# Fold, first column and product u in another order within the slots of a selective scan

## The chip, the cores and the metric

The kernel runs on one core of a Trainium2 chip. The metric is the device time of one execution in microseconds (us); less is better. The engines are named as in the profile: PE is TensorE (PEld are its weight loads), DVE is VectorE, ACT is ScalarE, POOL is GpSimd, and SP is SyncE, which here issues nearly all DMAs. Each engine works through its own instructions in order, and waits for others by semaphores.

## The reference: what is computed

Layer 0 takes x (16 images, 96 channels, 64 x 64): a 1x1 convolution, then in every 8x8 window the 9 nearest neighbours of each pixel by cosine distance, an edge convolution with gelu, a maximum over the neighbours, another 1x1 convolution and a residual. Layer 1 runs two Mamba blocks over the 4096 pixels of each image as a sequence, and then a fusion convolution, a batch norm and a residual. The part that the change touches is the selective scan of a Mamba block:

```
delta = softplus(dt @ dt_w + dt_b)                 # 192 channels
dA  = exp(delta[..., None] * A)                    # 16 states for each channel
dBx = delta[..., None] * B[:, :, None, :] * xc[..., None]
h_t = dA_t * h_(t-1) + dBx_t                       # over the sequence
y   = sum over states of h * C, plus Dp * xc
```

## The kernel before

Each image is cut into 8 rows of 512 pixels. Layer 0 works on one row at a time; a Mamba block (layer i = 0 or 1 of image b, row k) on such a row is an **item** n. There are 256 items, and the two blocks alternate, block 1 four rows behind block 0.

An item has 8 **slots**, p = 0 to 7, one for each pair of states: 128 partitions hold 64 channels for each of two states, and the free dimension holds 3 groups of channels times 512 pixels. There are 2048 slots; m counts them. In slot m the following is written, in this order, and each engine sees its own part of it in this order:

- PE: the **broadcast** of B for slot m + 1 into the one PSUM tile bt (`bcast`, L792). It must wait until the product of slot m has read bt.
- DVE: the **scan** of slot m (L990) over da and db into a tile hb, of which there are 3.
- All engines: one step of each generator that is under way. These hold layer 0 (`nearest`, `edges`), the norm and the projections of the item after next (`norm`, `prelude`), the start values of the next item (`carry`) and the end of the last one (`tail`). ACT's exponentials da (L758) and the DMAs of C (ct, L751) are written two slots ahead (`chosen`). PE writes products into two PSUM buffers that ACT must empty.
- In slot 7 only, POOL: `restart(*after)`, the first column for slot 0 of the next item.
- DVE: the **product** db = u * bt for slot m + 1 (`times_b`, L798).
- PE: the **fold** of slot m - 1 (`folded`, L814 and L816): it adds hb, already multiplied by C, into the item's y in PSUM. In slot 1 a new y is begun (`skipped`), and the fold of slot 0 is put off until behind the broadcast of slot 2.
- POOL: a copy of the last column of hb as state (L1024), then **hb times ct**, the product with C (L1025).
- POOL: `restart`, the **first column** of u for slot m + 2 (L789), in all slots but 6. It overwrites a column of u that the product of slot m + 1 reads, and the product of slot m + 2 needs it.

In slot 4 of an item the prelude of the item after next begins; in slot 4 of the following one it writes ACT's softplus (L720, L721) with the eight DMAs of delta (`doubled`), then POOL's **product u**, up = sp * xc (L732), and in slot 5 the eight DMAs that spread up into u. `carry` reads u in slot 7.

Waiting lists (`between`, `later`, `late`, `closing`, `opening`) hold steps of layer 0 for a fitting place in a slot. Nothing plans at run time: the order of every engine's instructions is fixed by the order in which Python writes them.

Of the kernel before, what the change touches and what calls it, by code (L numbers as in the profile page):

```python
# [14 lines left out]
ALU = mybir.AluOpType  # L15
# [6 lines left out]
def tile_conv_knn_mamba(ctx: ExitStack, tc: tile.TileContext, w: dict, out: bass.AP):  # L22
# [8 lines left out]
    nc = tc.nc  # L31
# [22 lines left out]
    NPR = NS // 2  # L54
# [270 lines left out]
    later = [[], []]  # L325
    late = []
# [9 lines left out]
    def half(h):  # L336
        return slice(h * CB, (h + 1) * CB)
# [7 lines left out]
    def close_steps():  # L345
        while closing:
            products, use = closing.pop(0)
            uses.append(partial(use, products()))

    def open_steps():  # L350
        for several in (uses, opening):
            while several:
                several.pop(0)()
# [230 lines left out]
    def pooled(b):  # L584

        mean = pr.tile([C, 1], F32, tag="mean1", name=f"mean1_{b}")
        nc.vector.reduce_sum(mean, means.pop(b), AX.X)
        yield
        pg = pm.tile([C, 1], F32, tag="mm", name=f"pg_{b}")
        nc.tensor.matmul(pg, lhsT=gpT, rhs=mean, start=True, stop=True)  # L590
        yield
        gp = pr.tile([C, 1], F32, tag="gp", name=f"gp_{b}")
        nc.scalar.activation(gp, pg, AF.Relu, bias=gp_b[:, 0, :], scale=1.0 / L)
        yield
        def product():
            ps = pm.tile([C, 1], F32, tag="mm", name=f"pg2_{b}")
            nc.tensor.matmul(ps, lhsT=fusT[:, 1, :], rhs=gp, start=True, stop=True)
            return ps

        apart(product, lambda ps: nc.scalar.copy(gcol[:, b : b + 1], ps))  # L600
        yield


    PIECES = ((0, 2), (2, NB3))
    LAG = 4
    NR = NB * NQ
# [13 lines left out]
    def norm(n):  # L620

        b, i, k = items[n]
        nm = f"{b}_{i}_{k}"
        seq = seqs[b, k]
        assert (b, k) in done
        hn = hns[n % NHN]
        if k == 0:
            nc.gpsimd.memset(hn[:, :HALO], 0.0)
        else:
            nc.gpsimd.tensor_copy(hn[:, :HALO], hns[place[b, i, k - 1] % NHN][:, Q:])  # L630
        pc = pm.tile([C, Q], F32, tag="mm", name=f"pc_{nm}")
        nc.tensor.matmul(pc, lhsT=cmat, rhs=seq, start=True, stop=True)
        sq = pr.tile([C, Q], F32, tag="sq", name=f"sqv_{nm}")
        nc.scalar.activation(sq, pc, AF.Square)  # L634
        yield
        ps = pm.tile([C, Q], F32, tag="mm", name=f"pvar_{nm}")
        nc.tensor.matmul(ps, lhsT=ones_cc, rhs=sq, start=True, stop=True)
        rs = pr.tile([C, Q], F32, tag="rs", name=f"rs_{nm}")
        nc.scalar.activation(rs, ps, AF.Ln, bias=eps_t[:C], scale=1.0 / C)
        nc.scalar.activation(rs, rs, AF.Exp, scale=-0.5)  # L640
        yield
        nc.gpsimd.tensor_tensor(hn[:C, HALO:], seq, rs, ALU.mult)

    def prelude(n):
# [5 lines left out]
        xc = pr.tile([128, Q + QH], F32, tag="xc", name=f"xc_{nm}")  # L650
# [58 lines left out]
        sp = pr.tile([128, Q + QH], F32, tag="sp", name=f"sp_{nm}", bufs=1)  # L709
# [16 lines left out]
        up = pr.tile([128, Q + QH], F32, tag="up", name=f"up_{nm}", bufs=1)  # L726
# [2 lines left out]
            yield  # L729
        while pressed:  # L730
            pressed.pop(0)()
        nc.gpsimd.tensor_tensor(up, sp, xc, ALU.mult)  # L732
        yield
        doubled(u, up)

# [51 lines left out]
    def restart(n, p):  # L787

        nc.gpsimd.tensor_copy(made[n][5][:, :, 0], carried[n][:, :, p])  # L789

    def bcast(n, p):
        nc.tensor.matmul(bt[:, 1:], lhsT=bsel[:, p, :], rhs=made[n][2][:, 1:], start=True, stop=True)  # L792

    def times_b(n, p):
        parts = []
        for lo, hi in PIECES:
            db = pd.tile([128, hi - lo, Q], F32, tag=f"db{lo}", name=f"db{lo}_{n}_{p}")
# [13 lines left out]
    def folded(n, p, hb, y):  # L811

        for h in range(2):
            nc.tensor.matmul(y[half(h), 0], lhsT=fold, rhs=hb[:, h, :], start=False, stop=(p == NPR - 1))  # L814
        for h in range(2):
            nc.tensor.matmul(  # L816
                y[half(h), 1, :QH], lhsT=fold, rhs=hb[:, 2, bass.ts(h, QH)], start=False, stop=(p == NPR - 1)
            )
# [44 lines left out]
    def drain(*several):  # L863

        several = list(several)
        while several:
            next(loading, None)
            open_steps()
            several = [g for g in several if next(g, several) is not several]
            close_steps()  # L870
            for rest in (*later, late):
                while rest:
                    rest.pop(0)()
        open_steps()
# [10 lines left out]
    def several_at_once(g, pace):  # L885

        while True:
            made = 0
            while made < pace:
                step = next(g, g)  # L890
                if step is g:
                    return
                if step in (TABLE, SLOT):
                    break
                made += step is not SPARE
            yield step
# [14 lines left out]
    order = [(n, p) for n in range(NI) for p in range(NPR)]  # L911
# [3 lines left out]
    def ahead():  # L915
        if coming:
            t = coming.popleft()
            soon[t] = chosen(*t)
# [24 lines left out]
    y = behind = None  # L943
# [7 lines left out]
    for m, (n, p) in enumerate(order):  # L951
        b, i, k = items[n]
        nm = f"{b}_{i}_{k}"
        after = order[m + 1] if m + 1 < len(order) else None

        for layer0, r, pace in rows_at.pop(m, ()):
            steps = layer0(*divmod(r, NQ))
            going.append(several_at_once(steps, pace) if pace > 1 else steps)
        between.extend(later[0])
        later = [later[1], []]  # L960
        if p == 0 and k == 0:
            states[i] = pr.tile([128, NB3, NPR], F32, tag=f"state{i}", name=f"state_{nm}")
        if p == 0 and whole:
            going.append(pooled(whole.pop(0)))
        if p == 0 and n + 2 < NI:
            going.insert(0, norm(n + 2))
        if p == 4 and n + 2 < NI:
            preps.append(prelude(n + 2))
        if p == 6 and n + 1 < NI:
            going.append(carry(n + 1))  # L970
        ct, at = soon.pop((n, p))
        if after is not None:
            bcast(*after)
        if p == 2:
            folded(*put_off)


        while uses:
            uses.pop(0)()
        acts = list(opening)  # L980
        opening.clear()
        if not acts and between and p not in (0, 1):
            acts.append(between.popleft())
        if len(acts) > 1:
            acts.pop(0)()
        for act in acts:
            act()
        hb = pr.tile([128, NB3, Q], F32, tag="hb", name=f"hb_{nm}_{p}", bufs=3)
        for (lo, hi), part in zip(PIECES, db):
            nc.vector.tensor_tensor_scan(  # L990
                *(t.rearrange("p c q -> p (c q)") for t in (hb[:, lo:hi], das[at][:, lo:hi], part)), 0.0, ALU.mult, ALU.add
            )
        free.append(at)
        while late:
            if between:
                between.popleft()()
            else:
                late.pop(0)()
        if p == 1 and n:
            yc = emptied(n - 1, y)  # L1000
        if p == 7 and n:
            going.append(tail(n - 1))
        if p == 2:
            ahead()
        held = step_on(going)
        if p == 4:
            ahead()
        held |= step_on(preps)
        close_steps()
        if between and p in (4, 5):  # L1010
            between.popleft()()
        if after is not None:
            if p == NPR - 1:
                restart(*after)
            db = times_b(*after)
        if behind is not None:
            if p == 1:
                y = py.tile([128, 2, Q], F32, tag="y", name=f"y_{nm}")
                skipped(n, y)
                put_off = (*behind, y)  # L1020
            else:
                folded(*behind, y)
        if k + 1 < NQ:
            nc.gpsimd.tensor_copy(states[i][:, :, p : p + 1], hb[:, :, Q - 1 : Q])  # L1024
        nc.gpsimd.tensor_tensor(hb, hb, ct.unsqueeze(1).to_broadcast([128, NB3, Q]), ALU.mult)  # L1025
        if m + 2 < len(order) and p != NPR - 2:
            restart(*order[m + 2])
        if p == 1 and n:
            gate(n - 1, yc)
        behind = (n, p, hb)  # L1030
        while (not held or not soon) and len(soon) < AHEAD and coming:
            ahead()
# [68 lines left out]
```

## Time and profile before

| what | value |
|---|---|
| median of 3 runs | 12,521.8 us (12,520.07 to 12,522.95) |
| the profiled execution | 12,521.96 us |
| its span, first to last instruction | 12,520.2 us |
| granted TensorE clock, mean | 0.984 |
| busy: ACT, POOL | 82%, 80% |
| hb times ct (L1025) | 2048 times, 3454 ns each |
| product u (L732) | 256 times, 1813 ns each; POOL idle before it 443.1 us |
| first column (L789) | 2047 times, 212 ns each |
| scan (L990) | 2048 pairs, 6944.1 us in all |

The span covers everything but 1.8 us of the profiled execution, and that execution is within 0.2 us of the median. A group's line in the profile has the number of instructions, their busy time and mean duration, and the idle time of their engine just before them with what ended it. The end of a PE instruction is modelled, so starts are the safer numbers there.

### The profile page before, as it was taken

What the parts mean: (1) busy time and instruction counts of PE and PEld (TensorE: products, weight loads), DVE (VectorE), ACT (ScalarE), POOL (GpSimd) and SP (SyncE); (2) the same over time, 40 slices, a digit from 0 to 9 for tenths busy, and PEclk for the clock granted to TensorE, in tenths of its full rate; (3) what the DMA queues carried; (4) which work ended last, traced back from release to release, by engine and by line L of the source; (5) the groups of instructions that cost most, each with busy time, mean ns of one, the idle gap of its engine ahead of it and who ended that gap; (6) DMA issues with size and microseconds to landing.
All of it is one profiled execution on the core that took longest, in us unless ns stands there. A gap on an engine that the chain in (4) does not pass through costs nothing. (4 is left out here: it accounts for less than half of the span.)

```text
span 12520.2 us, 169034 instructions
## 1 busy us (share of the span) xinstructions
PE 11019.7 (88%) x50504; PEld 4348.2 (35%) x50504; DVE 11646.8 (93%) x10589; ACT 10249.1 (82%) x16756; POOL 10022.4 (80%) x10148
## 2 busy tenths in 40 slices
PE   7989899898999999899999989989999898998972
PEld 2333333333333333333333333333333333333320
DVE  3999999999999999999999999999999999999995
ACT  6888888888888888888888888888888888888863
POOL 2888888888888888888888888888888888888882
PEclk9999999999999999999999999999999999999996
DMA  1333333333333333333333333333333333333336
GB/s 38 90 86 94 88 90 93 85 92 90 89 92 88 92 91 88 92 91 87 93 89 89 93 86 93 91 89 92 87 93 91 86 93 88 90 93 86 93 92 270
DMA packets 1221003, 1169.01 MB, mean 93 GB/s; under 512 B 631456, under 2 KB 762926, under 8 KB 1213936
## 3 DMA queue, kind: packets, MB, share of 16 engines
q1 hardware_dynamic: 1212720, 1132.88, 33.8%
q10 hardware_dynamic: 7360, 25.32, 0.5%
q8 instruction: 397, 6.50, 0.2%
q14 instruction: 526, 4.31, 0.1%
HBM read 640.79 MB, written 93.09 MB: 59 GB/s over the span
## 5 line engine op out<-in xcount | busy, mean ns | idle before, releaser
L1025 POOL TENSOR_TENSOR hb<-hb,ct 128x1536 f32<-128x1536 f32 x2048 | 7074.4, 3454 | 692.0 <-DMA ct<-cd 448.0
L990 DVE TENSOR_TENSOR_SCAN hb<-da,db 128x1024 f32<-128x1024 f32 (+1 forms) x4096 | 6944.1, 1738 | 4.2 <-ACT da L758 4.2
L798 DVE TENSOR_TENSOR db<-u,bt 128x1024 f32<-128x1024 f32 (+1 forms) x4096 | 3711.4, 952 | 564.1 <-PE bt L792 201.0
L758 ACT ACTIVATE da<-delta,a 128x511 f32<-128x511 f32 x6144 | 3946.1, 710 | 15.9 <-DVE hb L990 8.2
L814 PE MATMUL y<-hb,fold 128*64 128x512 f32 x8192 | 2179.7, 610 | 41.2 <-POOL hb L1025 41.2
L516 ACT ACTIVATE da<-t,eb,es 128x512 f32<-128x512 f32 x1536 | 1168.3, 776 | 714.0 <-PE t L508 453.3
L816 PE MATMUL y<-hb,fold 128*64 128x256 f32 x8192 | 1244.0, 382 | 0.0
L508 PE MATMUL t<-oh,vu 128*128 128x512 f32 x2048 | 1006.4, 613 | 28.2 <-ACT da L516 26.6
L816 PEld LDWEIGHTS y<-hb,fold 128*64 128x64 f32 x8192 | 593.0, 138 | 1191.2 <-issue 1191.2
L1024 POOL COPY state<-hb 128x3 f32<-128x3 f32 x1792 | 374.6, 209 | 766.4 <-DVE hb L990 731.0
L447 DVE TENSOR_REDUCE hq<-da 128x192 f32<-128x1536 f32 x512 | 891.6, 1742 | 91.3 <-ACT da L516 91.3
L792 PE MATMUL bt<-bparts,bsel 128*128 128x511 bf16 x2048 | 796.0, 389 | 180.0 <-DVE db L798 176.6
L659 PE MATMUL pj<-hn,conv_in 128*128 128x512 f32 x2048 | 934.7, 599 | 18.4 <-ACT gcol L600 8.8
L814 PEld LDWEIGHTS y<-hb,fold 128*64 128x64 f32 x8192 | 507.9, 137 | 1078.1 <-issue 695.3
L511 PE MATMUL t<-oh,vu 128*64 128x512 f32 x2048 | 560.8, 626 | 311.6 <-ACT da L516 309.0
L732 POOL TENSOR_TENSOR up<-sp,xc 128x768 f32<-128x768 f32 x256 | 464.1, 1813 | 443.1 <-ACT sp L721 442.9
L664 PE MATMUL pj<-hn,conv_in 128*64 128x256 f32 x4096 | 498.9, 385 | 259.0 <-ACT xc L671 258.8
L671 ACT ACTIVATE xc<-pj,conv_b 128x512 f32<-128x512 f32 (+1 forms) x512 | 297.0, 580 | 425.3 <-PE pj L664 400.4
L477 ACT ACTIVATE oh<-off 64x512 f32<-64x512 bf16 x1024 | 638.2, 623 | 6.4
L492 PE MATMUL pv<-ewT,y 96*64 96x192 f32 x2048 | 447.0, 342 | 143.8 <-ACT sqv L634 83.2
L659 PEld LDWEIGHTS pj<-hn,conv_in 128*128 128x128 f32 x2048 | 378.6, 190 | 406.0 <-issue 368.7
L508 PEld LDWEIGHTS t<-oh,vu 128*128 128x128 f32 x2048 | 371.9, 193 | 394.9 <-issue 298.5
(188 smaller groups left out, 15801.1 us busy)
## 6 DMA issues: line engine op xcount, KB each, us to landing
ct<-cd SPq DMA_DIRECT2D x4096, 128.0 KB
delta<-sp SPq DMA_DIRECT2D x1024, 128.0 KB
u<-up SPq DMA_DIRECT2D x1024, 128.0 KB
delta<-sp SPq DMA_DIRECT2D x1024, 64.0 KB
u<-up SPq DMA_DIRECT2D x1024, 64.0 KB
x<-in_x SPq DMA_DIRECT2D x128, 192.0 KB
rn<-r4d SPq DMA_DIRECT2D x128, 192.0 KB
x_d<-x SPq DMA_DIRECT2D x128, 192.0 KB
```

Of the source, the lines that this page charges most:

```text
L447: nc.vector.tensor_reduce(out(), g.rearrange("p s (i k) -> p s i k", k=KO), AX.X, ALU.max)
L477: nc.scalar.activation(ohs[p][0:NN, h], off[half(h)], AF.Relu, bias=1.0, scale=-1.0)
L508: nc.tensor.matmul(t, lhsT=vus[p][:, part, :128], rhs=ohw[part], start=True, stop=True)
L516: nc.scalar.activation(g, t, AF.Gelu, bias=e_b[:, j : j + 1], scale=e_s[:, j : j + 1])
L659: nc.tensor.matmul(ps, lhsT=wt[:, t, :128], rhs=hn[:, off : off + Q], start=(t == 0), stop=(t == taps - 1))
L758: nc.scalar.activation(da[:, c, 1:Q], delta[:, c, 1:], AF.Exp, scale=a_neg[i][:, c, p : p + 1])
L792: nc.tensor.matmul(bt[:, 1:], lhsT=bsel[:, p, :], rhs=made[n][2][:, 1:], start=True, stop=True)
L798: nc.vector.tensor_tensor(db, made[n][5][:, lo:hi], bt.unsqueeze(1).to_broadcast([128, hi - lo, Q]), ALU.mult)
L814: nc.tensor.matmul(y[half(h), 0], lhsT=fold, rhs=hb[:, h, :], start=False, stop=(p == NPR - 1))
L816: nc.tensor.matmul(y[half(h), 1, :QH], lhsT=fold, rhs=hb[:, 2, bass.ts(h, QH)], start=False, stop=(p == NPR - 1))
L990: nc.vector.tensor_tensor_scan(*(t.rearrange("p c q -> p (c q)") for t in (hb[:, lo:hi], das[at][:, lo:hi], part)), 0.0, ALU.mult, ALU.add)
L1025: nc.gpsimd.tensor_tensor(hb, hb, ct.unsqueeze(1).to_broadcast([128, NB3, Q]), ALU.mult)
```

## The change

Three things move; no instruction is added or taken away.

1. The fold is always put off: a slot's fold is no longer written behind the next slot's product but at the start of the slot after, behind the broadcast. `HASTE` holds all 16 places, so the branch that folds at once is left only for the last slot of the program. Slots 2 and 10 of every 16 had this order already.
2. In slots 0 to 4 and 7 the first column for slot m + 2 is written ahead of the state copy and of hb times ct. In slot 5 it stays behind them; slot 6 has none. The column of slot 7 for the next item's slot 0 stays where it was.
3. The product up = sp * xc is put on a list (`behindhand`) and written behind hb times ct of the same slot, behind the first column too. The start of the program, which prepares the first items in `drain`, empties the list at the end of each round.

```diff
+    HASTE = {0,1,2,3,4,5,6,7,8,9,10,11,12,13,14,15,}
+    put_off = []
+    behindhand = []
...
-        nc.gpsimd.tensor_tensor(up, sp, xc, ALU.mult)
+        behindhand.append(lambda: nc.gpsimd.tensor_tensor(up, sp, xc, ALU.mult))
         yield
         doubled(u, up)
...
-            for rest in (*later, late):
+            for rest in (behindhand, *later, late):
...
         if after is not None:
             bcast(*after)
-        if p == 2:
-            folded(*put_off)
-
+        while put_off:
+            folded(*put_off.pop())
...
                 skipped(n, y)
-                put_off = (*behind, y)
-            else:
-                folded(*behind, y)
+            put_off.append((*behind, y))
+            if p != 1 and (m % 16 not in HASTE or after is None):
+                folded(*put_off.pop())
+        if m + 2 < len(order) and p < NPR - 3 or p == NPR - 1 and after is not None:
+            restart(*order[m + 2])
         if k + 1 < NQ:
             nc.gpsimd.tensor_copy(states[i][:, :, p : p + 1], hb[:, :, Q - 1 : Q])
         nc.gpsimd.tensor_tensor(hb, hb, ct.unsqueeze(1).to_broadcast([128, NB3, Q]), ALU.mult)
-        if m + 2 < len(order) and p != NPR - 2:
+        if p == NPR - 3:
             restart(*order[m + 2])
+        while behindhand:
+            behindhand.pop(0)()
```

## Prediction

> **What bounds the kernel now.** I read the page first, for the busy shares and the costliest groups. They point at the vector engine: it is busy 93%, and its product db = u times bt, which starts the work of every slot, has sat idle 564.1 us before it.
>
> ```profile
> PE 11019.7 (88%) x50504; PEld 4348.2 (35%) x50504; DVE 11646.8 (93%) x10589; ACT 10249.1 (82%) x16756; POOL 10022.4 (80%) x10148
> L798 DVE TENSOR_TENSOR db<-u,bt 128x1024 f32<-128x1024 f32 (+1 forms) x4096 | 3711.4, 952 | 564.1 <-PE bt L792 201.0
> ```
>
> Next I read the timeline of the vector engine. The loop repeats every 16 slots (two items and one row of layer 0). I number slots 0 to 15 within such a period, and db(8) is the product for slot 8. Here are db(1), db(8) and the next db(1) of two periods; the idle time stands in brackets.
>
> ```profile
> 4038.84 1.83 DVE L798 TENSOR_TENSOR db<-u,bt 128x1024 f32<-128x1024 f32 x2 [2.12 <-PE bt L792]
> ...
> 4078.57 1.83 DVE L798 TENSOR_TENSOR db<-u,bt 128x1024 f32<-128x1024 f32 x2 [0.17 <-POOL u L789]
> ...
> 4132.81 1.83 DVE L798 TENSOR_TENSOR db<-u,bt 128x1024 f32<-128x1024 f32 x2 [2.12 <-PE bt L792]
> ```
>
> ```profile
> 4513.36 1.83 DVE L798 TENSOR_TENSOR db<-u,bt 128x1024 f32<-128x1024 f32 x2 [2.07 <-PE bt L792]
> ...
> 4554.63 1.83 DVE L798 TENSOR_TENSOR db<-u,bt 128x1024 f32<-128x1024 f32 x2 [1.71 <-POOL u L789]
> ...
> 4607.32 1.83 DVE L798 TENSOR_TENSOR db<-u,bt 128x1024 f32<-128x1024 f32 x2 [1.38 <-POOL b L698]
> ```
>
> The period is 93.97 us in the one and 93.96 in the other, although POOL held the vector engine up by 0.17 us at db(8) in the first and by 1.71 in the second; what is lost at db(8) is missing from the next wait at db(1). The broadcast for slot 9 starts 44.43 us after that for slot 1 in both, and in 9 of 10 of the 121 full periods within 0.02 of that. So something that neither the vector engine nor POOL moves sets the period: TensorE and ScalarE, which wait for each other. The timelines of both in slots 2 and 3 show it.
>
> ```profile
> 6127.57 0.38 PE L792 MATMUL bt<-bparts,bsel 128*128 128x511 bf16 x1
> 6127.88 1.08 PE L814 MATMUL y<-hb,fold 128*64 128x512 f32 x4
> 6128.79 0.60 PE L816 MATMUL y<-hb,fold 128*64 128x256 f32 x4
> 6129.32 1.98 PE L508 MATMUL t<-oh,vu 128*128 128x512 f32 x4
> 6132.65 1.08 PE L511 MATMUL t<-oh,vu 128*64 128x512 f32 x4 [1.34 <-ACT da L516]
> 6133.56 1.03 PE L814 MATMUL y<-hb,fold 128*64 128x512 f32 x4
> 6134.42 0.60 PE L816 MATMUL y<-hb,fold 128*64 128x256 f32 x4
> 6134.95 0.39 PE L792 MATMUL bt<-bparts,bsel 128*128 128x511 bf16 x1
> 6135.18 1.88 PE L508 MATMUL t<-oh,vu 128*128 128x512 f32 x4
> ```
>
> ```profile
> 6133.78 0.78 ACT L516 ACTIVATE da<-t,eb,es 128x512 f32<-128x512 f32 x1 [0.51 <-PE t L511]
> 6136.24 0.78 ACT L516 ACTIVATE da<-t,eb,es 128x512 f32<-128x512 f32 x1 [1.68 <-PE t L508]
> ```
>
> ScalarE idles 1.68 us because TensorE, between two products of layer 0, does a fold (L814, L816) and a broadcast (L792). The same 1.68 stands in slot 11. I followed the rest of that period (6,119 to 6,213 us) back from one broadcast to the next: each step is TensorE waiting for ScalarE, ScalarE waiting for TensorE, or either busy; no step waits for DVE or POOL. TensorE does wait 176.6 us in all for db (mostly in slots 10 and 15), but ScalarE is later still there.
>
> **Fold behind broadcast.** In slots 2 and 10 the kernel already has this order; 14 of 16 slots change. The work between two products of layer 0 is the same fold and broadcast, only swapped, so the cycle of TensorE and ScalarE gains nothing. The broadcast comes 1.39 us earlier (6133.56 to 6134.95), which takes DVE's waits for it away where it was late; but DVE then waits longer elsewhere, at the latest at the next db(1).
>
> The swap has a price. The rows above hold both orders. Old order: fold at 6133.56, L508 at 6135.18: 1.62 us. New order: broadcast at 6127.57, L508 at 6129.32: 1.75 us. The difference is one more step from the 128*128 to the 128*64 form: fold after broadcast starts 0.31 later (6127.57 to 6127.88), L508 after broadcast 0.23 later (6134.95 to 6135.18). A further step comes in ahead of the broadcast where the product before it is of the 64 form.
>
> ```profile
> 6181.49 1.08 PE L511 MATMUL t<-oh,vu 128*64 128x512 f32 x4
> 6182.50 1.13 PE L523 MATMUL ta<-y,ewT 96*128 96x512 f32 x2
> ```
>
> L511 ends at 6182.57 and the wide L523 starts 0.07 before that; the fold, of L511's own form, starts 0.17 before L511's end (6133.73 to 6133.56). So a broadcast behind L511 starts 0.10 later than a fold would, and L508 comes 0.10 + 1.75 - 1.62 = 0.23 us later than now. That holds in seven slots, which have a 64 form before and a wide one behind (1, 3, 4, 6, 11, 14, 15). In five of them TensorE then waits for ScalarE anyway (0.35 to 1.37 us in the period I followed). Slots 3 and 11 are on the cycle, at the two waits of 1.68. Cost: 2 x 0.23 x 121 periods = 56 us. The bounds are 0 (if the steps hide) and seven slots, 7 x 0.23 x 121 = 195; I take two because only there ScalarE waits for exactly this.
>
> The Trainium skill, TensorEngine Tiling (Array Packing), Key Properties, speaks against this edit: changing the tiling mode drains TensorE. The rows agree with about 0.1 us a change; the page gives no figure, so no other sum follows from it.
>
> **Broadcast that waits.** A broadcast cannot start before DVE has read the old bt. Now the fold fills such a wait; afterwards it stands behind it, and with it all of the slot's products on TensorE, for which ScalarE waits. TensorE would be ready for the broadcast of slot 9 at 44.43 - 1.45 = 42.98 us after that of slot 1; db(8) must end before, so begin before about 41.1. It can't begin earlier than now, because its first column is late behind a chain of POOL and DMA that the change leaves alone. In 38 of 121 periods it begins later, by 15.7 us in all. I charge 16; the bounds are 0 and 36 (counting from 40.7, where the broadcast of slot 10 starts to wait). Slots with DVE ahead don't pay.
>
> **First column ahead of the product with C** (POOL, slots 0 to 4 and 7). Removed is the wait of db behind 3.45 us of hb times ct (L1025), some 146 us in all by my count of waits that end with the first column; of those, the 83 at db(8) stay, since that column is written in slot 7 as before. Added is a wait: the column must wait for the next db, and queued behind it on POOL are the state copy and hb times ct, which now start some 2 us after the scan. POOL's work of 10022.4/128 = 78 us a period fits into 94. Walking one period, every hb is still ready before its fold; the least margin is slot 7's, 1.2 us (hb ends 52.57, fold 53.74 on that walk), and there ct's landing sets it, not the column. So 0 inside the period; its cover is these margins, and each us beyond them would go onto the cycle.
>
> **Product u behind.** up (1.81 us, once per item) leaves its place ahead of the state copy, where POOL waits 442.9 us for ScalarE's softplus. It ends some 5 us later: behind the wait for db(5), the state copy and 3.45 us of hb. Its eight DMAs stand on SP behind delta's eight and ct's, and start 8.7 and 6.8 us after the old up's end in the two items of the period that I walked, so the later up still comes first, by 1.5 us at the least. Cost 0; without that cover, ct behind it on SP would be late, 1 us for 1 us.
>
> **The tail** (after 11,900 us, layer 0 is done) has no such cycle, and there POOL's order decides:
>
> ```profile
> 12094.29 1.83 DVE L798 TENSOR_TENSOR db<-u,bt 128x1024 f32<-128x1024 f32 x2 [2.78 <-POOL u L789]
> ```
>
> Thirteen such waits make 20.3 us. Column first and up later take most away; u then lands late for slot 7, about 0.9 us each time. I take 12 off; bounds 0 and 20.
>
> **Sum.** The profiled execution took 12,521.96 us (span 12,520.2; median of the runs 12,521.8). 12,522 + 56 + 16 - 12 = 12,582, rounded to 12,580. By the bounds that have ground (0 to 56 for the swap, up to 36 for broadcasts, tail 0 to 20) the case with a priced swap reaches from 12,548 to about 12,615; I let it go to 12,640 for other slots of the seven that run out of cover.
>
> **Rivals.** (1) The swap costs nothing because the steps hide: 12,522 - 12 = 12,510, with the waiting broadcasts up to 12,546. For it: TensorE overlaps weight loads; against it: the 1.75 that stands in slots 2 and 10. (2) The other side: DVE is the bound after all, and its waits for broadcast and column go. By the waits that makes up to 379 + 146 = 525 us, 11,997; half of it gives 12,260. It needs 4 us of slack per period in TensorE and ScalarE; it decides as soon as the broadcast of slot 9 moves nearer than 44.43 to that of slot 1. Against it: the fixed 93.96 us. The skill's Trace Analysis page (Perfetto Trace Analysis, Identifying the Most-Contended Engine) would pick the engine with the highest occupancy, here DVE, and so this rival; the constant period speaks against it. (3) POOL's added wait makes folds late: 1 us in each period beyond the 1.2 of slot 7 is 121 us, 12,700.
>
> **Chances.** Forecast 0.58, (1) 0.22, (2) 0.14, (3) 0.06. The range 12,497 to 12,640 holds the first two. What a measurement can tell from no change is 0.2%, 25 us: faster 0.14 (rival 2), same 0.22 (rival 1), slower 0.64.
>
> **What would show it.** Right: period near 94.4 us; ScalarE's two waits of 1.68 grown to about 1.9; DVE's waits for the broadcast moved, and their sum hardly less; POOL's wait for softplus gone, a new one for db. Wrong: a period under 93.9, or TensorE waiting for hb in the folds.

## The result, and the profile after

The changed kernel takes **12,694.45 us** (median; 12,688.13 to 12,703.5), the kernel before 12,520.93 us in the runs beside it. The ratio is 1.0139, with a 95% interval of 1.0126 to 1.0151. The forecast was 12,580 in a range up to 12,640: the direction was right, the loss of some 173 us is three times the 58 that were forecast. The profiled execution took 12,692.99 us (span 12,691.3), 171 more than that of before.

First the page of after: the busy times, and the groups that answer to those read before. In after the broadcast is L795, db L801, the fold L817 and L819, the first column L792 and product u L735; L508, L511 and L516 keep their numbers.

```profile
PE 11349.9 (89%) x50504; PEld 4252.2 (34%) x50504; DVE 11737.4 (92%) x10589; ACT 10261.9 (81%) x16756; POOL 10025.9 (79%) x10148
...
L801 DVE TENSOR_TENSOR db<-u,bt 128x1024 f32<-128x1024 f32 (+1 forms) x4096 | 3714.7, 952 | 611.6 <-POOL u L792 270.4
...
L792 POOL COPY u<-fresh 128x3 f32<-128x3 f32 x2047 | 475.6, 232 | 1455.5 <-DVE db L801 1396.6
...
L735 POOL TENSOR_TENSOR up<-sp,xc 128x768 f32<-128x768 f32 x256 | 464.4, 1814 | 15.6 <-ACT sp L724 15.6
```

DVE's idle time before db has not fallen; it has risen from 564.1 to 611.6 us. POOL's wait for softplus (443.1 us before product u) is down to 15.6, and in its place the first column waits 1396.6 us for db. So the change moved on POOL what it was to move, and the time got longer all the same. TensorE has the same 50,504 instructions and 330 us more of busy time, by its modelled ends. DVE is busy 91 us longer with the same instructions; 56 us of that are one line of layer 0 (L549, 1564 ns each instead of 1125).

Next the list of waits: in each line the time in all, the number of waits and the longest. First before, then after.

```profile
ACT da L516 <- PE t L508: 453.3, 281, 3.3
...
ACT sqv L634 <- PE pc L632: 255.6, 146, 2.0
...
PE bt L792 <- DVE db L798: 176.6, 190, 3.4
```

```profile
ACT da L516 <- PE t L508: 544.5, 273, 4.0
...
ACT sqv L637 <- PE pc L635: 299.8, 192, 2.1
...
PE bt L795 <- DVE db L801: 229.3, 350, 4.0
```

ScalarE waits 91 us longer for layer 0's product L508 and 44 us longer for pc; TensorE waits for db 350 times instead of 190. The timeline shows the first of these. These are TensorE and ScalarE of after in slots 2 and 3 of a period, the place that was shown of before:

```profile
6117.11 1.08 PE L511 MATMUL t<-oh,vu 128*64 128x512 f32 x4 [1.34 <-ACT da L516]
6118.12 0.39 PE L795 MATMUL bt<-bparts,bsel 128*128 128x511 bf16 x1
6118.44 1.08 PE L817 MATMUL y<-hb,fold 128*64 128x512 f32 x4
6119.35 0.60 PE L819 MATMUL y<-hb,fold 128*64 128x256 f32 x4
6119.88 1.98 PE L508 MATMUL t<-oh,vu 128*128 128x512 f32 x4
```

```profile
6118.24 0.78 ACT L516 ACTIVATE da<-t,eb,es 128x512 f32<-128x512 f32 x1 [0.51 <-PE t L511]
6121.05 1.64 ACT L516 ACTIVATE da<-t,eb,es 128x512 f32<-128x512 f32 x2 [2.03 <-PE t L508]
```

The wait of 1.68 us is now 2.03: 0.35 more, not the 0.23 of the forecast. It is 2.03 in slot 3 of all 121 periods, and in slot 11 of 97.

To see where all of the loss lies I put the two traces' 16,756 ScalarE instructions, which come in the same order, side by side, and took by how much each step to the next start grew, summed over the 121 periods. The sum is 159.4 us; the rest of the 171 lies behind and ahead of the periods.

| part | forecast | measured |
|---|---|---|
| ScalarE's waits for L508 in slots 3 and 11 | +56 | 42.2 + 53.5 = +96 |
| slots 8 and 9, waits for pc (+30.9), pvar (+14.5) and pv (-10.1) | +16 | +35 |
| the end of the period (pow, L849: +11.5), pc in slot 0 (+10.5) and small ones | 0 | +28 |
| tail | -12 | +9 |
| start and end | 0 | +3 |
| sum | +60 | +171 |

### The profile page after: what moved, and what is told of

It reads as the page before. It is cut to its first block, busy times and chain, and to the rows that moved or that the text cites. A ratio compares the mean times of both kernels' runs of the same rounds, so it can differ in the third digit from the quotient of the medians.

```text
span 12691.3 us, 168938 instructions
## 1 busy us (share of the span) xinstructions
PE 11349.9 (89%) x50504; PEld 4252.2 (34%) x50504; DVE 11737.4 (92%) x10589; ACT 10261.9 (81%) x16756; POOL 10025.9 (79%) x10148
## 4 chain that ended last, share of the span: by engine, by line
ACT 24%; PE 23%; POOL 21%; issue 10%; SPq 10%; DMA 7%; DVE 4%; POOLq 0%; ACTq 0%; DVEq 0%
POOL hb L1029 15%; ACT da L761 10%; SPq L745 3%; SPq L743 3%; PE y L817 3%; DMA ct<-cd 3%; SPq L754 3%; PE t L511 3%; DVE db L801 3%; PE t L508 2%; ACT L723 1%; DMA r4d<-r 1%; ACT da L516 1%; PE pj L667 1%; PE y L819 1%
## 5 line engine op out<-in xcount | busy, mean ns | idle before, releaser
L801 DVE TENSOR_TENSOR db<-u,bt 128x1024 f32<-128x1024 f32 (+1 forms) x4096 | 3714.7, 952 | 611.6 <-POOL u L792 270.4
L817 PE MATMUL y<-hb,fold 128*64 128x512 f32 x8192 | 2242.2, 626 | 3.7 <-POOL hb L1029 3.4
L516 ACT ACTIVATE da<-t,eb,es 128x512 f32<-128x512 f32 x1536 | 1168.6, 776 | 811.3 <-PE t L508 544.5
L792 POOL COPY u<-fresh 128x3 f32<-128x3 f32 x2047 | 475.6, 232 | 1455.5 <-DVE db L801 1396.6
L819 PE MATMUL y<-hb,fold 128*64 128x256 f32 x8192 | 1245.7, 383 | 0.0
L508 PE MATMUL t<-oh,vu 128*128 128x512 f32 x2048 | 1031.7, 625 | 35.9 <-ACT da L516 34.3
L795 PE MATMUL bt<-bparts,bsel 128*128 128x511 bf16 x2048 | 791.8, 387 | 244.0 <-DVE db L801 229.3
L819 PEld LDWEIGHTS y<-hb,fold 128*64 128x64 f32 x8192 | 594.9, 139 | 1194.1 <-issue 1194.1
L662 PE MATMUL pj<-hn,conv_in 128*128 128x512 f32 x2048 | 949.3, 606 | 20.1 <-ACT gcol L600 10.1
L511 PE MATMUL t<-oh,vu 128*64 128x512 f32 x2048 | 564.9, 630 | 366.9 <-ACT da L516 364.2
L817 PEld LDWEIGHTS y<-hb,fold 128*64 128x64 f32 x8192 | 408.8, 136 | 1083.1 <-issue 642.6
L508 PEld LDWEIGHTS t<-oh,vu 128*128 128x128 f32 x2048 | 348.7, 191 | 493.2 <-issue 415.9
L735 POOL TENSOR_TENSOR up<-sp,xc 128x768 f32<-128x768 f32 x256 | 464.4, 1814 | 15.6 <-ACT sp L724 15.6
```

Of the source, the lines that this page charges most:

```text
L508: nc.tensor.matmul(t, lhsT=vus[p][:, part, :128], rhs=ohw[part], start=True, stop=True)
L511: nc.tensor.matmul(t[half(h)], lhsT=vus[p][:, h, 128:], rhs=ohw[h], start=True, stop=True)
L516: nc.scalar.activation(g, t, AF.Gelu, bias=e_b[:, j : j + 1], scale=e_s[:, j : j + 1])
L662: nc.tensor.matmul(ps, lhsT=wt[:, t, :128], rhs=hn[:, off : off + Q], start=(t == 0), stop=(t == taps - 1))
L801: nc.vector.tensor_tensor(db, made[n][5][:, lo:hi], bt.unsqueeze(1).to_broadcast([128, hi - lo, Q]), ALU.mult)
L819: nc.tensor.matmul(y[half(h), 1, :QH], lhsT=fold, rhs=hb[:, 2, bass.ts(h, QH)], start=False, stop=(p == NPR - 1))
```

## Experiments

**The three parts alone.** Theory: the loss comes from the folds alone; the other two parts are off the cycle.

> Only the folds are put off (all 16 places); first column and product u stand where the kernel before has them. Theory A (cycle of TensorE and ScalarE: after the change ScalarE's two waits of 1.68 us for L508 are 2.03, 0.35 us each, 85 us over 121 periods; most of the rest comes from broadcasts that wait for the product of DVE with the fold behind them): 12,640 to 12,690, nearly all of the loss. Rival B (POOL: the first column that waits for db, 1396.6 us of waits in the changed kernel, makes hb times ct and so the folds late): 12,500 to 12,550, since the column isn't moved here.

> Only the first column is written ahead of hb times ct (slots 0 to 4 and 7). Theory A: no step of the cycle waits for POOL, so the period stays 93.96 us and only the tail gains some: 12,505 to 12,535, although POOL waits some 1,000 us more for db. Rival B: most of the 172 us, 12,620 or more.

> Only the product u is written behind hb times ct. Theory A: period unchanged, tail a little shorter: 12,505 to 12,535. Rival B' (u lands later, carry and the first column of the next item with it): 12,560 or more, with DVE's wait at db(8) grown by 0.5 us or more.

The main lines of the edits, each made in the kernel before (what else each takes over from the change, such as the lists and `put_off.append`, is left out here):

```diff
folds_alone:
-        if p == 2:
-            folded(*put_off)
+        while put_off:
+            folded(*put_off.pop())
column_alone:
+        if m + 2 < len(order) and p < NPR - 3 or p == NPR - 1 and after is not None:
+            restart(*order[m + 2])
product_alone:
-        nc.gpsimd.tensor_tensor(up, sp, xc, ALU.mult)
+        behindhand.append(lambda: nc.gpsimd.tensor_tensor(up, sp, xc, ALU.mult))
```

| kernel | us | ratio to before |
|---|---|---|
| folds alone | 12,738.27 | 1.0177 [1.0160, 1.0194] |
| column alone | 12,528.00 | 1.0009 [0.9999, 1.0018] |
| product alone | 12,514.49 | 0.9999 [0.9989, 1.0008] |

The folds carry all of the loss and more, 48 us above the range that was expected. Column and product alone move nothing that the intervals tell from 1, although they do what they were written for. With the column alone DVE's wait for the column falls and its wait for the broadcast rises (131.3 and 201.0 us before; here the waits of that kernel):

```profile
DVE db L798 <- PE bt L792: 310.1, 254, 11.2
DVE db L798 <- POOL u L789: 107.4, 121, 5.5
```

One wait of DVE has been exchanged for another (all its idle time before db is 561.0 us, against 564.1), and the period stays: 93.98 us against 93.96 (medians). An engine off the cycle waits for it, whichever of its inputs comes last.

**Which folds?** Slots 3 and 11 get the old order back.

> The changed kernel, but in slots 3 and 11 the fold stands ahead of the broadcast again (14 of 16 places put off instead of 16). Theory A: ScalarE's two waits for L508 go back from 2.03 to 1.68, which is 85 us: 12,590 to 12,620. Rival C (each of the 14 swaps costs TensorE its share, 172/14 = 12 us): 12,670.

```diff
-    HASTE = {0,1,2,3,4,5,6,7,8,9,10,11,12,13,14,15,}
+    HASTE = set(range(16)) - {2, 10}
```

Measured: 12,613.91 us, ratio 1.0077 [1.0062, 1.0092], 80.5 us less than the change, as 2 x 0.35 x 121 = 85 has it. In its timeline ScalarE's wait is back:

```profile
6084.73 1.64 ACT L516 ACTIVATE da<-t,eb,es 128x512 f32<-128x512 f32 x2 [1.68 <-PE t L508]
```

So half of the loss comes from two of the 14 swaps. The other half must be in the rest: its ScalarE still waits 45.7 us more for pc in slot 8, and 16.3 for pvar in slot 9.

**Five slots old.**

> The changed kernel with five folds back ahead of their broadcast: the two of slots 3 and 11, and those at the broadcasts of slots 9, 10 and 0 (HASTE without 2, 7, 8, 10, 14). Theory A: there the broadcast waits for the product of DVE, and the fold now stands behind that wait (ScalarE's longer waits for the products that follow, pc in slot 8, the variance in slot 9 and the output product at the end of the period, make 45.7 + 16.3 - 10.5 + 12.4 = 64 us with folds_but_two): back to 12,520 to 12,550, so nearly all of folds_but_two's 98 us goes. Rival C (what is left is a price of each remaining swap): 9 of 12 swaps stay, 12,590.

```diff
+    HASTE = set(range(16)) - {2, 7, 8, 10, 14}
```

Measured: 12,544.15 us, ratio 1.0020 [1.0011, 1.0029]: all but 25 us of the loss is gone, with nine of the 14 changed slots still in the new order. Its median period is 94.04 us. The folds of slots 8, 9 and 15 carry the other half, and the remaining nine swaps, with column and product moved too, cost no more than those 25 us.

**Why 0.35 and not 0.23?** First the two swaps alone in the kernel before, then the same with the broadcast split into two products of 64 columns, the form that the fold has. If the time goes into steps between the forms, that step is gone and the wait falls.

> The kernel before, with only the folds of slots 3 and 11 put behind their broadcast. Theory A: ScalarE's two waits of 1.68 become 2.03, nothing else moves: 2 x 0.35 x 121 = 85 us, 12,600. Rival D (the waits only move, DVE has the broadcast 1.4 us earlier there and uses it): 12,500 to 12,520.

> As folds_two_alone, and every broadcast is made of two products of 64 columns each, in the same 128*64 form as the fold, instead of one of 128*128. Theory A (the price of the swap is the change of form, about 0.1 us each): two of three changes go, between the product ahead and the broadcast and between broadcast and fold, ScalarE's waits are 1.83 instead of 2.03, 12,550. Rival E (the price lies in the order, the fold's first weights can't be loaded ahead behind a broadcast): 2.03 stays, 12,600 or more.

```diff
folds_two_alone, in the kernel before:
+    HASTE = {2, 10}
...
folds_two_halves, on top of it:
-        nc.tensor.matmul(bt[:, 1:], lhsT=bsel[:, p, :], rhs=made[n][2][:, 1:], start=True, stop=True)
+        for h in range(2):
+            nc.tensor.matmul(
+                bt[half(h), 1:], lhsT=bsel[:, p, half(h)], rhs=made[n][2][:, 1:], start=True, stop=True
+            )
```

Two swaps alone took 12,642.33 us (ratio 1.0098 [1.0083, 1.0113]), 123 more than before and 40 more than the theory expected. Slot 3 fits: the wait is 2.03 us in all 121 periods, 42.15 us in all. Slot 11 doesn't: only 33 waits are 2.03, and in the others TensorE's broadcast comes late, since it waits for db, with ScalarE behind it. ScalarE loses some 75 us there.

```profile
ACT da L516 <- PE t L508: 582.3, 290, 3.9
...
PE bt L794 <- DVE db L800: 263.2, 259, 3.8
```

With halves it took 12,603.84 us (1.0070 [1.0054, 1.0087]): 38.5 less. By its total this fits the rival's number better than the theory's, but only because the total carries slot 11's waits for db. So I asked the same again in the changed kernel, where slot 11 is nearly free of them.

> The changed kernel, with each broadcast as two products of 64 columns (form 128*64, as the folds) in place of one of 128. In folds_two_halves this took ScalarE's waits for L508 from 2.03 to 1.77 us. Theory A: the same here in slots 3 and 11, so 2 x 0.26 x 121 = 63 us less than the change's 12,694 us: about 12,631, and a little less still if the other steps between forms cost too. Rival E: the 0.35 us of a swap is not a matter of forms, or the second product gives it all back: 12,680 or more.

The edit is the split above, in the changed kernel. Measured: 12,627.83 us, ratio 1.0084 [1.0067, 1.0101], **66.6 us less than the change**, where 63 were expected. In the traces ScalarE's steps in slots 3 and 11 fall by 31 and 36 us, and others grow by 16. Its TensorE and ScalarE in slots 2 and 3:

```profile
6100.39 1.08 PE L511 MATMUL t<-oh,vu 128*64 128x512 f32 x4 [1.37 <-ACT da L516]
6101.29 0.39 PE L796 MATMUL bt<-bparts,bsel 128*64 128x511 bf16 x2
6101.51 1.03 PE L820 MATMUL y<-hb,fold 128*64 128x512 f32 x4
6102.37 0.60 PE L822 MATMUL y<-hb,fold 128*64 128x256 f32 x4
6102.90 1.98 PE L508 MATMUL t<-oh,vu 128*128 128x512 f32 x4
```

```profile
6104.06 1.64 ACT L516 ACTIVATE da<-t,eb,es 128x512 f32<-128x512 f32 x2 [1.77 <-PE t L508]
```

The broadcast starts 0.90 behind L511's first start instead of 1.01, the fold 0.22 behind the broadcast instead of 0.32, and the wait is 1.77 instead of 2.03. So 0.26 of the 0.35 us goes with the steps between forms. The other 0.09 to 0.10 is the L508 group itself: it shows 1.98 here and in the change, and 1.88 where the broadcast is directly ahead of it (6135.18 in before). Its first product takes 0.53 us to the next start instead of 0.43, by the medians over the 121 periods. That step stood in the rows that I had quoted: 1.98 in slot 2, 1.88 in slot 3.

**What gives the 44 us back?** Folds alone took 12,738 us, all three parts 12,694.

> All folds behind the broadcast and the first column early; product u at its old place. Folds alone took 12,738 us, all three parts 12,694. Theory A: the 44 us that the other two parts give back come from the first column, because with the folds behind, the column of slots 0 to 4 and 7 was behind hb times ct and held up db (353 us of such waits with folds alone, 270 with all three parts), and so the next broadcast: about 12,695. Rival G: they come from product u, whose old place held POOL 707 us for softplus: about 12,738. Rival H: only both together: between 12,715 and 12,738.

> All folds behind the broadcast and product u behind hb times ct; the first column at its old place. Theory A: the column gives the 44 us back, so this stays at about 12,735. Rival G: product u does, since then hb times ct no longer starts behind the wait for softplus (707 us with folds alone): about 12,695. Rival H: between 12,715 and 12,735.

The edits are the parts shown above, two at a time. Folds and column took 12,710.52 us (1.0155 [1.0140, 1.0170]), folds and product 12,725.62 (1.0168 [1.0152, 1.0183]). The column gives back 28 us and both together 44; the four runs of each of these kernels lie clear of those with the folds alone (12,729 to 12,739). The 13 us of the product are not shown: its runs lie at 12,710 to 12,737. So the theory had the larger part right, and whether product u gives the rest is open. Where a fold stands behind the broadcast, a db that comes late is not covered any more, and what makes db early has a value that it didn't have by itself.

**Is it a cycle of TensorE and ScalarE?** If it is, work on TensorE that is taken out of ScalarE's waits must shorten the kernel, with DVE and POOL unchanged. The folds of slots 3 and 11 are moved forward, between the products L508 and L511 of slots 2 and 10, where TensorE waits for ScalarE 1.34 and 0.66 us in the period that I followed.

> The kernel before, with the folds of slots 3 and 11 moved forward instead of back: written between L508 and L511 of the first of the two products of layer 0 (slots 2 and 10), where TensorE waits 1.34 and 0.66 us for ScalarE. Theory A: the fold's 1.4 us fill that wait and leave the cycle; L511 comes 0.1 and 0.8 later, L508 after it 1.4 earlier, so the period falls by about 1.3 + 0.6 us, 200 to 230 us in all: 12,290 to 12,330. Rival B (DVE or POOL sets the period): 12,480 or more.

```diff
                 for part in range(3):
+                    if part == 2:
+                        while fill:
+                            folded(*fill.pop())
...
+        if p == 2 and behind is not None:
+            fill.append((*behind, y))
         held = step_on(going)
...
-            else:
+            elif p != 2:
                 folded(*behind, y)
+            while fill:
+                folded(*fill.pop())
```

Measured: **12,252.51 us, ratio 0.9786 [0.9772, 0.9801]**, faster than both kernels, by 267 us against before and by some 40 more than expected. In its TensorE the fold (here L818 and L820) fills the wait ahead of the product of form 128*64 (here L514), and between that and the next wide one (here L511) only the broadcast is left. ScalarE waits 0.39 us instead of 1.68:

```profile
5905.31 1.98 PE L511 MATMUL t<-oh,vu 128*128 128x512 f32 x4
5907.22 1.08 PE L818 MATMUL y<-hb,fold 128*64 128x512 f32 x4
5908.13 0.60 PE L820 MATMUL y<-hb,fold 128*64 128x256 f32 x4
5908.64 1.08 PE L514 MATMUL t<-oh,vu 128*64 128x512 f32 x4
5909.65 0.39 PE L796 MATMUL bt<-bparts,bsel 128*128 128x511 bf16 x1
5909.88 1.88 PE L511 MATMUL t<-oh,vu 128*128 128x512 f32 x4
```

```profile
5909.77 0.78 ACT L519 ACTIVATE da<-t,eb,es 128x512 f32<-128x512 f32 x1 [0.51 <-PE t L514]
5910.94 1.64 ACT L519 ACTIVATE da<-t,eb,es 128x512 f32<-128x512 f32 x2 [0.39 <-PE t L511]
```

The median period falls from 93.96 to 91.79 us, and DVE, whose work is the same, is busy 95% where it had been 93%. Side by side with before, ScalarE's steps in slots 3 and 11 are 156 and 158 us shorter and those in slot 10 are 51 longer, which leaves nearly the whole of the 261 us that the periods lose. An earlier broadcast for DVE is not the reason: it starts 1.01 us behind the first product of form 128*64, in before 2.30, but 1.01 is also what the change has in its rows above, and there the time got longer. That settles the cycle.

**Column and product in the shorter cycle.**

> The kernel before with the folds of slots 3 and 11 moved forward into ScalarE's wait (12,252 us by itself), and the first column early and product u behind as in the change; all other folds at their old places. Theory A: even in the shorter cycle of 91.8 us neither DVE nor POOL is on it, so both parts cost and gain nothing in the loop, and the tail gets up to 12 us longer: 12,245 to 12,270. Rival F: in the shorter cycle DVE's 139 us of waits for the first column lie on the path, and the two parts gain what they could not gain before: 12,120 to 12,220.

The edit is the one above with column_alone and product_alone. Measured: 12,255.70 us, 0.9795 [0.9778, 0.9811]: no difference to the fill by itself. DVE's wait for the column falls from 139.4 to 85.3 us, and its wait for the broadcast rises from 108.2 to 148.1. Even here the two parts of the change are off the path.

## Why the prediction was right or wrong

**What bounds the kernel: right.** TensorE and ScalarE waiting for each other set the period. The 2.1% of the fill, which removes nothing from DVE or POOL, shows it, and the rival "DVE is the bound after all" fell: with column and product alone the time stayed (1.0009 and 0.9999; the intervals reach 1.0018), and with the column its waits were exchanged.

**Fold behind broadcast: its two places right, the size too small; this step failed first.** It charged "0.10 + 1.75 - 1.62 = 0.23 us" in slots 3 and 11. From L511's last product to L508's first it is 2.041 us before and 2.286 after (medians): 0.245, which fits. But L508's first product then takes 0.53 us instead of 0.43, and I had counted only up to its start. 2 x 0.35 x 121 = 85 us, as folds_but_two shows (80.5). The other 11 us of the 96 in the table lie in slot 11, where some waits grew by more. That the other slots of the seven cost little was right for four of them: folds_but_five keeps the swaps of slots 1, 4, 6 and 14 and loses 25 us. Slot 15 it puts back too, so the run doesn't price that one. A third place I had at nothing, outside the seven: ScalarE's wait for pc in slot 0, 1.95 us in before and 2.01 or more in after in nearly every period, 10.5 us in all. The swap in that slot stands in folds_but_five too, and so does the wait of 2.01.

**Broadcast that waits: the mechanism was right, the slot and the size were not.** I charged 16 us, for the broadcast of slot 9 waiting for db(8). That one waits only 7.4 us in all. Its neighbours wait longer: the broadcast of slot 8, written in slot 7, 16.6 us for db(7) and 10.8 for the DMAs of u (1.4 in all before), that of slot 10 30.7 us (1.3 before), that of slot 0 of the next period, in slot 15, 72.6 us (15.0 before). Only that of slot 11 waits less, 17.1 instead of 106.0 us. Here is a place in slots 7 and 8 of after: DVE gets u late, TensorE's broadcast waits for db, the fold is queued behind it, and pc comes late for ScalarE.

```profile
11514.18 1.83 DVE L801 TENSOR_TENSOR db<-u,bt 128x1024 f32<-128x1024 f32 x2 [2.19 <-POOL u L792]
```

```profile
11516.06 0.38 PE L795 MATMUL bt<-bparts,bsel 128*128 128x511 bf16 x1 [1.07 <-DVE db L801]
11516.36 1.08 PE L817 MATMUL y<-hb,fold 128*64 128x512 f32 x4
11517.27 0.60 PE L819 MATMUL y<-hb,fold 128*64 128x256 f32 x4
...
11522.58 0.38 PE L795 MATMUL bt<-bparts,bsel 128*128 128x511 bf16 x1 [0.34 <-DVE db L801]
11522.89 1.08 PE L817 MATMUL y<-hb,fold 128*64 128x512 f32 x4
11523.79 0.60 PE L819 MATMUL y<-hb,fold 128*64 128x256 f32 x4
11524.33 1.10 PE L635 MATMUL pc<-x,cmat 96*96 96x512 f32 x2
```

```profile
11525.46 0.59 ACT L637 ACTIVATE sqv<-pc 96x512 f32<-96x512 f32 x1 [1.17 <-PE pc L635]
```

In before TensorE had a cover there: it waited for ScalarE (off, L471) in 120 of 121 periods, 87.0 us in all. In after 25.1 are left, 86 times: what TensorE loses ahead of it uses the cover up, and where nothing is left of it ScalarE waits. That other slots "run out of cover" I had only in the range.

**First column and product u: right that they cost nothing by themselves.** POOL's added waits delay no fold: over the periods no fold waits for hb, and over the whole run they wait 3.4 us, so the rival with POOL at 12,700 us is wrong, though its number lies near the result. What I missed is that they aren't independent of the folds: behind swapped folds the two together give back 44 us.

**Tail: wrong sign.** I took 12 us off; it costs 9. The waits for the column did go (18.5 to 5.4 us), and others took their place. The broadcast of one slot in each item is queued behind a projection that waits for ScalarE's softplus. In before that broadcast ended only 0.2 to 0.5 us ahead of the late column in six of the column's waits, which make 12.9 us of the 20.3 that I had added up; so of these 12.9 little could be gained. Two more of the thirteen, 2.8 us, had ended with the broadcast itself. TensorE and DVE of after:

```profile
12254.31 3.70 PE L662 MATMUL pj<-hn,conv_in 128*128 128x512 f32 x8 [1.44 <-ACT sp L723]
12257.85 0.38 PE L795 MATMUL bt<-bparts,bsel 128*128 128x511 bf16 x1
```

```profile
12258.32 1.83 DVE L801 TENSOR_TENSOR db<-u,bt 128x1024 f32<-128x1024 f32 x2 [2.71 <-PE bt L795]
```

With the column alone the tail loses 12 us (and the periods gain as much) by another way: the column waits for db, hb times ct starts behind it, and the fold, still ahead of the broadcast, waits for hb. POOL and TensorE of column_alone:

```profile
12101.03 0.19 POOL L789 COPY u<-fresh 128x3 f32<-128x3 f32 x1 [2.28 <-DVE db L798]
...
12101.43 3.43 POOL L1027 TENSOR_TENSOR hb<-hb,ct 128x1536 f32<-128x1536 f32 x1
```

```profile
12104.91 1.08 PE L814 MATMUL y<-hb,fold 128*64 128x512 f32 x4 [1.86 <-POOL hb L1027]
```

That is rival 3's mechanism; it exists, but only where layer 0 no longer sets the pace.

**What stays open.** The 28 us of small terms: the largest, at pow, goes with the five swaps that folds_but_five leaves out, and stands behind the broadcast written in slot 15 that now waits for db; of the 10.5 us at pc in slot 0, 7.7 stay there. I didn't follow each of the others. Nor did I follow whether the longer L549 on DVE delays a db for which a broadcast then waits. Between 300 and 11,800 us the granted clock is at 0.5 for 68 us in before and for 99 in after. If all 121 periods had grown by the 1.21 us of the 91 that have no such stretch in either trace, the sum would be 146; so 13 of the 159 us stand there. Whether TensorE's denser work brings these stretches on is not shown: folds_two_alone is slower than before and has 48 us of them.

## What to carry to other kernels

Before an engine's waits are worked on, look for a period that stays fixed while that engine's waits move: where it does, an edit that exchanges one wait of the engine for another is worth nothing, and the pair whose waits end in each other is the place to edit. A reorder of equal work on TensorE is priced up to the end of the group that the next engine waits for, steps between forms and the first product behind them included, and it pays or costs only where that group is waited for. A fixed order that puts work behind a waiting instruction takes away cover that the old order had; the better edit was the opposite one, to move such work forward into a wait that is there in every period.

## What the hardware showed

- A step between a 128*128 product and 128*64 ones costs about 0.10 us on TensorE: the fold starts 0.32 us behind a broadcast of form 128*128, and 0.22 behind one split into two of 128*64. The two halves of the split broadcast start within 0.01 us of each other, so the split itself took no time that shows here.
- The first wide f32 product behind a fold takes 0.53 us to the next start, behind a broadcast 0.43. I had not expected a price inside the group, and no run here shows what causes it.
- The Trainium skill, TensorEngine Tiling (Array Packing), Key Properties, says that changing the tiling mode drains TensorE. The runs agree as far as the steps go, and give them a size here: 0.26 us for each swap that added them. The drain itself is not seen in a trace.
